# Seven products of quarters move from the second expert layer to the first, in a fixed order; V products and query pairs take turns

## The chip, the cores and the metric

The kernel runs on one core of one Trainium2 chip. A core has five engines that run side by side, each through its own list of instructions in order, and wait for each other by semaphores: TensorE (PE, the matmuls; PEld is its loading of the stationary operand), VectorE (DVE), ScalarE (ACT), GpSimd (POOL) and SyncE (SP, which here only starts transfers). The metric is the device time of one execution in microseconds (us), and a profiled execution gives a trace of every instruction.

## What is computed

Four sequences of 1024 tokens of width 256 (f32) go through a gated cross attention to 64 context tokens and a gated mixture of experts:

```python
x = x + tanh(g_xattn[0]) * xattn(layernorm(x), ctx, ctx, ...)
x = x + tanh(g_ffn[0]) * moe(layernorm(x), gate_w, w1, w2)

# xattn: 16 heads of 64
qh, kh, vh = (einsum('bld,hdk->hblk', t, w) for t, w in ((q, w_qs), (k, w_ks), (v, w_vs)))
attn = softmax(einsum('hblk,hbmk->hblm', qh, kh))
out = einsum('hblm,hbmk->hblk', attn, vh) * qh      # times the query once more
return concat_heads(out) @ w_proj.T + b_proj

# moe: 8 experts, F = 1024, the best two of each token
w_topk, sel = top_k(xt @ gate_w.T, 2); w_topk = softmax(w_topk)
h = silu(xt @ w1[e]); y = h @ w2[e]                 # for the chosen experts
out = sum over the two of w_topk * y
```

## The kernel before

**Attention.** The 4096 tokens are eight groups g of 512, each four tiles t of 128. The main loop goes over groups and tiles; at each tile it computes scores and softmax of the tile (`probabilities`), transposes the probabilities of the tile before, and does a share of the work of other groups: at t = 1 the V products of the group before (`attend`, matmuls L469 into PSUM tiles po, which VectorE multiplies by the query, L478) and then that tile's list of head pairs of the next group's queries (`queries`, matmuls L408 into pq, copied out by ScalarE, L416). `attend` works on two head pairs at a time, which take two PSUM banks. All these PSUM tiles come from one pool of four banks (`ps1`), used in turn; a pool of two tiles of two banks each (`ps2`) holds scores. In groups 2 to 6 two head pairs of queries stand at t = 1, in group 1 one, in 7 and 8 none.

**Experts.** Rows of tokens, sorted by expert, lie in a table in DRAM. They are worked off in slots; one slot has one expert's weights and so many rows. Slots 0 to 8 hold 256 tokens of the first half of the sequence and run partly beside attention. Slots 9 to 19 are wide: 9 to 14 ("sixes") hold 384 tokens, 15 to 19 ("fives") 320. Slots 20 to 28 hold 256 again. For each slot s, `run_slots` issues in this order: the first layer (`hidden`, L954 and L962: 8 blocks of F, two chunks of the contraction, Silu on ScalarE), the transpose of the tokens of slot s+1 (L928, VectorE), the second layer of slot s-1 (`combine`), the sums for slot s's own second layer (`quarter_sums`), and the loads of the weights of s+3 and the tokens of s+4 (SyncE's queue). An f32 matmul is two instructions in the trace. First-layer outputs use `ps2`, second-layer outputs `ps1`.

`combine` first makes the ids of the rows and their weights (L1040, L1043, VectorE, from small transfers that come with the tokens), multiplies, scales by the token's weight (L1088) and adds the rows to the output by a scatter of POOL (L1073). For the slots that `by_quarters` names (9 to 26) the product of two blocks of 128 tokens is done by seven products of quarters instead of eight (the Winograd form of Strassen's scheme): VectorE makes four sums of the hidden values (sh) and four of the weights (sw), each 128x512 (L987); `pair_of_blocks` does seven products of 128 columns (L1000), and the sums of products are made while leaving PSUM, on VectorE (L1010) and ScalarE (L1015, L1025). A third block of a wide slot is done plainly (L1109).

**What sets the order.** The program is written with a framework that inserts the semaphores and that may move instructions of an engine by priority and expected readiness. `pinned` (with a true second argument, or none) keeps an instruction in the order in which pinned instructions were written. Before, the expert layers aren't pinned. SBUF blocks come from three rings, "group" (8), "weight" (7) and "hidden" (2 buffers), and a new holder of a buffer waits for the last reader of the old. `kept` are eight long-lived tiles of input rows; slots put their token rows and their scaled results in them.

Of the kernel before, what the change touches and what calls it, by code (L numbers as in the profile page):

```python
# [8 lines left out]
F32 = mybir.dt.float32  # L9
# [6 lines left out]
P = 128  # L16
# [5 lines left out]
def kernel(  # L22
# [900 lines left out]
    def transposed(s, xin):  # L923
        blocks = xin.shape[1]
        n = S + HALF if is_half(s) else blocks * P
        pool, tag = (rows, "xT") if blocks == 2 else (npool, "nT")
        xT = pool.tile([P, NC, n], F32, tag=tag, name=f"xT_{s}")
        nc.vector.transpose(  # L928
            xT.rearrange("p c (i j) -> p i c j", j=Q),
            xin.rearrange("p t (i m c) -> p (t i) c m", c=NC, m=Q)[:, : n // Q],  # L930
        )
        return xT

    def hidden(s, a, xT):
# [27 lines left out]
            nc.scalar.activation(hT[f0 // per_tile][:, f1 : f1 + step, :], ph, AF.Silu)  # L962
            yield hT

    attention_ends = False

    def by_quarters(s):
        return NA <= s < NA + OFTEN - 2

    def quarter_sums(s, b, hT):  # L970

# [62 lines left out]
    def combine(s, ids, b, y, hT, sums):  # L1034

        blocks = ids.shape[1]
        n = tokens_of(s)
        of_rows = ids.bitcast(I32)
        with behind_sums():
            nc.vector.tensor_tensor(  # L1040
                of_rows[:, :, 0, 1:2], of_rows[:, :, 0, 1:2], of_rows[:, :, 1, 0:1], ALU.min
            )
            nc.vector.tensor_tensor(ids[:, :, 0, 0:1], ids[:, :, 0, 0:1], ids[:, :, 1, 1:2], ALU.add)  # L1043
            if is_half(s):
                half_row = of_rows[:, 2, 0, 1:2]
                nc.vector.tensor_tensor(half_row, half_row, half_row, ALU.add)
                nc.vector.tensor_tensor(half_row, half_row, second_half, ALU.add)
        behind = [f"slot{s - 1}"] if s else ["out0"]
        if s == NA:
            behind.append("out1")  # L1050
        gathered = None
        if s == NA + OFTEN - 1:
            gathered = flat[0]
            for t in range(blocks):
                gather = nc.gpsimd.indirect_dma_start(
                    out=gathered[:, t],
                    out_offset=None,
                    in_=outf[:n],
                    in_offset=bass.IndirectOffsetOnAxis(ap=of_rows[:, t, 0, 1:2], axis=0),
                    bounds_check=n - 1,  # L1060
                    oob_is_err=False,
                )
                apart("out", gather, behind=behind)

        def width(t):
            return D // 2 if t == 2 and is_half(s) else D

        def scatter(t):

            w = width(t)  # L1070
            rows_of = n * D // w
            with behind_softmax():
                rows_added = nc.gpsimd.indirect_dma_start(  # L1073
                    out=outf.rearrange("n (h d) -> (n h) d", d=w)[:rows_of],
                    out_offset=bass.IndirectOffsetOnAxis(ap=of_rows[:, t, 0, 1:2], axis=0),
                    in_=y[:, t, :w],
                    in_offset=None,
                    bounds_check=rows_of - 1,
                    oob_is_err=False,
                    compute_op=ALU.bypass if gathered is not None else ALU.add,  # L1080
                )
            apart("out", rows_added, f"slot{s}", behind=behind)

        def add(t):

            weight = ids[:, t, 0, 0:1]
            if gathered is None:
                nc.vector.tensor_scalar(y[:, t, : width(t)], py[t], weight, None, ALU.mult)  # L1088
            else:
                nc.vector.scalar_tensor_tensor(y[:, t], py[t], weight, gathered[:, t], ALU.mult, ALU.add)  # L1090
            scatter(t)

        each = attention_ends
        per_tile = NF // len(hT)
        alone = range(blocks)
        if sums:
            yield from pair_of_blocks(s, ids, y, sums, scatter)
            alone = range(2, blocks)
        if attention_ends:
            py = {t: bank(f"py_{s}_{t}")[:, : width(t)] for t in alone}  # L1100
        else:
            both = bank(f"py_{s}").rearrange("p (t d) -> p t d", d=D)
            py = [both[:, t, :] for t in range(blocks)]
        for t in alone:
            w = width(t)
            m = P * w // D
            for f in range(NF):
                for i in range(D // w):
                    nc.tensor.matmul(  # L1109
                        py[t][i * m : (i + 1) * m],  # L1110
                        hT[f // per_tile][:, f % per_tile, t * P : t * P + m],
                        b[:, f, i * w : (i + 1) * w],
                        start=(f == 0),
                        stop=(f == NF - 1),
                    )
            if each:
                add(t)
            yield
        if not each:
            for t in range(blocks):  # L1120
                add(t)
# [2 lines left out]

    def run_slots(slots):

        ahead = 3
        issued.clear()
        tokens, weights = {}, {}

        def load(s):
            if s in slots:
                weights[s] = load_weights(s)

        def load_next(s):
            if s in slots:
                tokens[s] = load_tokens(s)

        for s in slots[:ahead]:
            load(s)  # L1140
            load_next(s)
        load_next(slots[0] + ahead)
        yield
        yield
        xT = transposed(slots[0], tokens[slots[0]][1])
        yield
        pending = None
        for s in slots:
            a, b = weights.pop(s)
            ids, xin = tokens.pop(s)  # L1150
            if s == slots[-1] and pending:
                yield from combine(*pending)
                pending = None
            for hT in hidden(s, a, xT):
                yield
            if s + 1 in slots:
                xT = transposed(s + 1, tokens[s + 1][1])
                yield
            if pending:
                yield from combine(*pending)  # L1160
            pending = (s, ids, b, xin, hT, quarter_sums(s, b, hT) if by_quarters(s) else None)
            load(s + ahead)
            load_next(s + ahead + 1)
        yield from combine(*pending)


# [16 lines left out]
    def finish(g, step):  # L1183

        qT, aT = held[g]
        if step == 1:
            attend(g, range(NP // 2, NP), qT, aT)
        elif step >= 2:
            project(g, qT, (step - 2) * 2)

    def leave(g):
# [58 lines left out]
    for g in range(NG + 1):  # L1250
# [7 lines left out]
        for t in range(T):  # L1258
            if t == 0 and g >= 2:
                leave(g - 2)  # L1260
            if g < NG:
                pr = probabilities(g, t, qT)
            if last:
                transpose_probabilities(*last)

            b = (g - GB - 1) // GB
            ends, behind = b * GB + GB - 1, (g - GB - 1) % GB * T + t if b >= 0 else -1
            if behind == T:
                placing(ends)
            if g and t == 1:  # L1270
                attend(g - 1, range(NP // 2), *held[g - 1])
            for h, pairs in parts[g].items():
                queries(h, qTs[h], pairs[t])
            if 0 <= g - 1 < NG:
                finish(g - 1, t)
            last = (g, t, pr, aT) if g < NG else None
            if g == 0:
                for _ in range(value_parts[t]):
                    next(pending_values)
            if behind >= 0:  # L1280
                after(ends, behind)
            if g == 0 and t == 1:
                tc.keep_in_program_order(nc.scalar.activation(tg, tg, AF.Tanh))
                tc.keep_in_program_order(
                    nc.gpsimd.tensor_scalar(bias, bias, tg[:, 0:1], None, ALU.mult)
                )
                for h in range(2):
                    add_bias(h)
            if g + 2 < NG:
                if t == 0 and (g + 2) % GB == 0:  # L1290
                    stats = ln_stats(list(range(g + 2, g + 2 + GB)), f"a{g + 2}")
                elif t == 2:
                    ln_norm(g + 2, stats, "a")
                    add_bias(g + 2)
            if g < 2:
                clear(g * T + t, 2 * T)
            for _ in range(pieces[g][t] if g in pieces else 0):
                next(slots)
# [53 lines left out]
```

## Time and profile before

| | |
|---|---|
| median of 3 runs | 864.3 us (864.23 to 866.57) |
| profiled execution | 863.83 us, span 862.1 us |
| TensorE busy | 837.9 us (97%), 4684 instructions |
| VectorE / ScalarE / GpSimd busy | 462.6 / 237.7 / 269.2 us |
| first layer L954 | 928 instructions, 237.4 us |
| plain second layer L1109 | 608 instructions, 109.6 us |
| V products, multiply L478 | 64 of 128x512, 676 ns each |

Busy times of one engine's parts overlap with other engines', so only the engine that has no free time sets the end. A row of a group gives the number of its instructions, the summed busy time, the mean of one and the idle time of the engine just before them with what ended it; since matmuls are pipelined, the mean of one matmul is longer than the step to the next. The chain of waits lists, for an engine, which instruction of which other engine it waited for. The attention part ends about 450 us into the span; the wide slots fill TensorE from 521 to about 740 us.

### The profile page before, as it was taken

What the parts mean: (1) busy time and instruction counts of PE and PEld (TensorE: products, weight loads), DVE (VectorE), ACT (ScalarE), POOL (GpSimd) and SP (SyncE); (2) the same over time, 40 slices, a digit from 0 to 9 for tenths busy, and PEclk for the clock granted to TensorE, in tenths of its full rate; (3) what the DMA queues carried; (4) which work ended last, traced back from release to release, by engine and by line L of the source; (5) the groups of instructions that cost most, each with busy time, mean ns of one, the idle gap of its engine ahead of it and who ended that gap; (6) DMA issues with size and microseconds to landing.
All of it is one profiled execution on the core that took longest, in us unless ns stands there. A gap on an engine that the chain in (4) does not pass through costs nothing. (4 is left out here: it accounts for less than half of the span.)

```text
span 862.1 us, 13243 instructions
## 1 busy us (share of the span) xinstructions
PE 837.9 (97%) x4684; PEld 655.4 (76%) x4684; DVE 462.6 (54%) x1136; ACT 237.7 (28%) x380; POOL 269.2 (31%) x216
## 2 busy tenths in 40 slices
PE   8999999999999999899999999999999999999995
PEld 5556858576776758687888887777778888999995
DVE  4466384769647985864138611454344643645520
ACT  2673242333332231542113010212121211221210
POOL 3042212213731164215423722222222232223132
PEclk9999999999999999999999999999999999999999
DMA  9999999401200044336765888775555837856611
GB/s 197 334 341 340 340 345 340 132 2 43 74 32 1 25 159 115 115 79 210 207 192 138 219 207 195 209 175 133 136 129 136 234 91 177 232 130 183 172 23 38
DMA packets 165032, 141.79 MB, mean 164 GB/s; under 512 B 72685, under 2 KB 159076, under 8 KB 161248
## 3 DMA queue, kind: packets, MB, share of 16 engines
q1 hardware_dynamic: 145456, 118.79, 47.3%
q0 software_dynamic: 12912, 17.11, 10.2%
q10 hardware_dynamic: 6592, 4.98, 1.8%
q8 instruction: 39, 0.64, 0.3%
q14 instruction: 33, 0.27, 0.1%
HBM read 78.73 MB, written 62.46 MB: 164 GB/s over the span
## 5 line engine op out<-in xcount | busy, mean ns | idle before, releaser
L954 PE MATMUL ph<-xT,w 128*128 128x256 f32 (+2 forms) x928 | 237.4, 412 | 0.4 <-ACT hT L962 0.3
L954 PEld LDWEIGHTS ph<-xT,w 128*128 128x128 f32 x928 | 174.2, 190 | 51.9 <-issue 1.9
L1073 POOL DMA_INDIRECT out_dram<-x,ids x69 | 111.4, 1614 | 287.5 <-DVE x L1010 127.9
L962 ACT ACTIVATE hT<-ph 128x1024 f32<-128x1024 f32 (+3 forms) x84 | 70.1, 847 | 249.2 <-PE ph L954 211.9
L443 POOL TENSOR_TENSOR pr<-pr,sm 128x1024 f32<-128x1024 f32 x32 | 61.4, 1918 | 208.2 <-DVE sm L441 143.8
L408 PE MATMUL pq<-nT_a,wq 128*128 128x512 f32 x256 | 116.2, 597 | 5.7 <-DVE qT L478 5.4
L486 PE MATMUL pp<-wp,qT 128*128 128x256 f32 x512 | 113.1, 379 | 0.0
L486 PEld LDWEIGHTS pp<-wp,qT 128*128 128x128 f32 x512 | 97.1, 190 | 18.2 <-issue 5.7
L1109 PE MATMUL py<-w,hT 128*128 128x256 f32 (+1 forms) x608 | 109.6, 352 | 0.0
L1109 PEld LDWEIGHTS py<-w,hT 128*128 128x128 f32 (+1 forms) x608 | 93.1, 176 | 12.0
L408 PEld LDWEIGHTS pq<-nT_a,wq 128*128 128x128 f32 x256 | 46.2, 190 | 58.3 <-issue 43.8
L606 POOL DMA_INDIRECT table<-x,to_row x64 | 63.1, 985 | 42.7 <-DVE x L595 24.8
L424 PEld LDWEIGHTS sc<-keys,qT 128*128 128x128 f32 x512 | 62.6, 192 | 11.2 <-issue 10.8
L424 PE MATMUL sc<-keys,qT 128*128 128x128 f32 x512 | 67.1, 278 | 0.0
L455 ACT COPY aT<-pa 128x512 f32<-128x512 f32 x64 | 34.4, 591 | 82.1 <-PE pa L454 72.2
L433 DVE TENSOR_REDUCE mx<-sc 128x16 f32<-128x1024 f32 x32 | 39.0, 1217 | 28.0 <-PE sc L424 27.9
L440 DVE TENSOR_REDUCE sm<-pr 128x16 f32<-128x1024 f32 x32 | 39.0, 1218 | 23.9 <-ACT pr L438 23.8
L1000 PE MATMUL q<-sw,sh 128*128 128x128 f32 x432 | 51.7, 275 | 0.0
L1000 PEld LDWEIGHTS q<-sw,sh 128*128 128x128 f32 x432 | 50.2, 192 | 0.8
L1088 DVE TENSOR_SCALAR x<-py,ids 128x256 f32<-128x256 f32 (+1 forms) x31 | 14.2, 459 | 63.1 <-PE py L1109 63.1
L416 ACT COPY qT<-pq 128x512 f32<-128x512 f32 x64 | 36.4, 581 | 35.3 <-PE pq L408 35.1
L478 DVE TENSOR_TENSOR qT<-po,qT 128x512 f32<-128x512 f32 x64 | 40.6, 676 | 5.7 <-PE po L469 5.7
(261 smaller groups left out, 853.8 us busy)
## 6 DMA issues: line engine op xcount, KB each, us to landing
w<-in_L_ffn_w_dram SPq DMA_DIRECT2D x58, 1024.0 KB
table<-empty SPq DMA_DIRECT2D x8, 5016.0 KB
x<-table SPq DMA_DIRECT2D x116, 64.0 KB
out_dram<-x ACTq DMA_DIRECT2D x8, 512.0 KB
x<-in_x_dram SPq DMA_DIRECT2D x7, 512.0 KB
out_dram<-x,ids POOLq DMA_INDIRECT x69, 4.1
wq<-in_L_xattn_w_qs_dram SPq DMA_DIRECT2D x4, 256.0 KB
wv<-in_L_xattn_w_vs_dram SPq DMA_DIRECT2D x2, 512.0 KB
```

Of the source, the lines that this page charges most:

```text
L408: product = nc.tensor.matmul(pq, wq[:, c, p * P : (p + 1) * P], nT[g][:, c, :], start=(c == 0), stop=(c == NC - 1),)
L424: nc.tensor.matmul(sc[:, p // 2, :, p % 2, :], of_pair(qT, p)[:, t * P : (t + 1) * P], kT[g // GB][:, p, :], start=True, stop=True,)
L433: nc.vector.tensor_reduce(mx, scv, AX.X, ALU.max)
L443: nc.gpsimd.tensor_tensor(pr, pr, sm.unsqueeze(2).to_broadcast([P, H, M]), ALU.mult).ins,
L478: nc.vector.tensor_tensor(own, po[j], own, ALU.mult)
L486: nc.tensor.matmul(pp[:, i, :], of_pair(qT, p)[:, t * P : (t + 1) * P], wp[:, p, :], start=(p == 0), stop=(p == NP - 1),)
L606: nc.gpsimd.indirect_dma_start(out=table.rearrange("r (u w) -> (r u) w", w=2), out_offset=bass.IndirectOffsetOnAxis(ap=to_row[:, k, i : i ...
L954: nc.tensor.matmul(ph[:, i, :], a[:, c, f * P : (f + 1) * P], xT[:, c, :], start=(c == 0), stop=(c == NC - 1),)
L962: nc.scalar.activation(hT[f0 // per_tile][:, f1 : f1 + step, :], ph, AF.Silu)
L1000: nc.tensor.matmul(to, left[:, f, :], right[:, f, :], start=not onto and f == 0, stop=f == NF // 2 - 1, skip_group_check=onto,)
L1073: rows_added = nc.gpsimd.indirect_dma_start(out=outf.rearrange("n (h d) -> (n h) d", d=w)[:rows_of], out_offset=bass.IndirectOffsetOnAxis( ...
L1109: nc.tensor.matmul(py[t][i * m : (i + 1) * m], hT[f // per_tile][:, f % per_tile, t * P : t * P + m], b[:, f, i * w : (i + 1) * w], start= ...
```

## The change

1. The first layer of the wide slots (9 to 19) is done by seven products of quarters. `first_sums`, called right behind the transpose of the slot's tokens, makes four sums of weights (128x512, into a block of the "weight" ring) and four of tokens (128x192 or 128x160, into `kept[0]` or `kept[1]` in turn). `hidden_by_quarters` then works in two groups of four of the eight blocks of F; in each, seven products with half the tokens as columns go into four banks (two tiles of `ps2`), one copy on ScalarE and five additions on VectorE join them, and four Silu on ScalarE write the hidden values. The second group's first products reuse the first group's banks.
2. The second layer of the wide slots is plain; quarters remain there for slots 20 to 26.
3. In the wide slots the instructions of TensorE, the transposes, the additions and sums, the Silu and the scalings are pinned: their order on each engine is as written.
4. In attention, at t = 1, each two head pairs of V products are followed by one head pair of queries, so that po01, po23, pqA, pqB becomes po01, pqA, po23, pqB; po45 and po67 follow at t = 1 as well. Before, these were issued by `finish` behind the queries.

```diff
@@ transposed @@
-        nc.vector.transpose(
+        turn = nc.vector.transpose(
...
+        pinned(turn, in_order)
@@ new functions behind hidden @@
+    def first_sums(s, a, xT):
+        half = NF // 2 * P
+        sa = block([P, 4, half], f"sa_{s}", "weight")
+        w = [[a[:, c, f * half : (f + 1) * half] for c in range(NC)] for f in range(2)]
+        h = xT.shape[2] // 2
+        sx = kept[(s + 1) % 2][:, : 4 * h].rearrange("p (q n) -> p q n", n=h)
+        x = [[xT[:, c, t * h : (t + 1) * h] for t in range(2)] for c in range(NC)]
+        for out_, in0, in1, op in (
+            (sa[:, 0], w[1][0], w[1][1], ALU.add),
+            (sa[:, 1], sa[:, 0], w[0][0], ALU.subtract),
+            (sx[:, 0], x[0][1], x[0][0], ALU.subtract),
+            (sx[:, 1], x[1][1], sx[:, 0], ALU.subtract),
+            (sa[:, 2], w[0][0], w[1][0], ALU.subtract),
+            (sx[:, 2], x[1][1], x[0][1], ALU.subtract),
+            (sa[:, 3], w[0][1], sa[:, 1], ALU.subtract),
+            (sx[:, 3], x[1][0], sx[:, 1], ALU.subtract),
+        ):
+            pinned(nc.vector.tensor_tensor(out_, in0, in1, op), in_order)
+        return w, x, sa, sx
+
+    def hidden_by_quarters(s, n, sums):
+        w, x, sa, sx = sums
+        h = n // 2
+        share = "hidden" if s > NA and (s - NA) % 2 == 0 else "group"
+        hT = [block([P, NF // 2, n], f"hT_{s}_{i}", share) for i in range(2)]
+        per = 2
+        for f0 in range(0, NF // 2, per):
+            banks = [ps2.tile([P, 2, 512], F32, tag="ps2", name=f"ph_{s}_{f0}_{i}") for i in range(2)]
+            q = [banks[i // 2][:, i % 2, : per * h].rearrange("p (f n) -> p f n", n=h) for i in range(4)]
+            u = soft.tile([P, 2, per * h], F32, tag="pr", name=f"u_{s}_{f0}")
...
+            product(q[0], w[0][0], x[0][0])
+            pinned(nc.scalar.copy(u2, q[0]))
+            product(q[1], sa[:, 1], sx[:, 1])
+            plus(u2, q[1], u2)
+            product(q[2], sa[:, 2], sx[:, 2])
+            plus(u3, q[2], u2)
+            product(q[3], sa[:, 0], sx[:, 0])
+            plus(to[1][1], q[3], u3)
+            leave_hidden(1, 1)
+            product(q[0], w[0][1], x[1][0], True)
+            leave_hidden(0, 0, q[0])
+            product(q[2], w[1][1], sx[:, 3], True)
+            plus(to[1][0], q[2], u2)
+            leave_hidden(1, 0)
+            product(q[3], sa[:, 3], x[1][1], True)
+            plus(to[0][1], q[3], u2)
+            leave_hidden(0, 1)
+            yield hT
@@ by_quarters @@
-        return NA <= s < NA + OFTEN - 2
+        return NA + NW <= s < NA + OFTEN - 2
@@ combine: scalings and plain products @@
+                pinned(scaled, in_order)
...
+                    pinned(product, in_order)
@@ run_slots @@
+            in_order = is_wide(s)
-            for hT in hidden(s, a, xT):
+            for hT in hidden_by_quarters(s, xT.shape[2], first) if first else hidden(s, a, xT):
                 yield
+            first = None
             if s + 1 in slots:
                 xT = transposed(s + 1, tokens[s + 1][1])
+                if is_wide(s + 1):
+                    first = first_sums(s + 1, weights[s + 1][0], xT)
@@ finish and the main loop @@
-        if step == 1:
-            attend(g, range(NP // 2, NP), qT, aT)
-        elif step >= 2:
+        if step >= 2:
...
-            if g and t == 1:
-                attend(g - 1, range(NP // 2), *held[g - 1])
-            for h, pairs in parts[g].items():
-                queries(h, qTs[h], pairs[t])
+            asked = [(h, p) for h, pairs in parts[g].items() for p in pairs[t]]
+            for q in range(NP // 2):
+                if g and t == 1:
+                    attend(g - 1, range(2 * q, 2 * q + 2), *held[g - 1])
+                for h, p in asked[q : q + 1] if q + 1 < NP // 2 else asked[q:]:
+                    queries(h, qTs[h], [p])
```

More of the change, by code (lines that the diff above doesn't have):

```diff
@@ L963, in hidden @@
             yield hT
-    attention_ends = False
+    attention_ends = in_order = False
+    def first_sums(s, a, xT):
[17 more added lines that the diff above has]
+        return w, x, sa, sx
@@ new lines, in hidden_by_quarters, with product, plus, leave_hidden @@
+    def hidden_by_quarters(s, n, sums):
[8 more added lines that the diff above has]
+            u = soft.tile([P, 2, per * h], F32, tag="pr", name=f"u_{s}_{f0}")
+            u2, u3 = (u[:, i].rearrange("p (f n) -> p f n", n=h) for i in range(2))
+            to = [[hT[f][:, f0 : f0 + per, t * h : (t + 1) * h] for t in range(2)] for f in range(2)]
+            def product(to, left, right, onto=False):
+                for f in range(per):
+                    pinned(
+                        nc.tensor.matmul(
+                            to[:, f, :],
+                            left[:, (f0 + f) * P : (f0 + f + 1) * P],
+                            right,
+                            start=not onto and f == 0,
+                            stop=True,
+                            skip_group_check=onto or f > 0,
+                        )
+                    )
+            def plus(to, of, other):
+                pinned(nc.vector.tensor_tensor(to, of, other, ALU.add))
+            def leave_hidden(f, t, of=None):
+                pinned(nc.scalar.activation(to[f][t], to[f][t] if of is None else of, AF.Silu))
+            product(q[0], w[0][0], x[0][0])
[16 more added lines that the diff above has]
+            yield hT
@@ L1087, in add @@
             if gathered is None:
-                nc.vector.tensor_scalar(y[:, t, : width(t)], py[t], weight, None, ALU.mult)
+                scaled = nc.vector.tensor_scalar(y[:, t, : width(t)], py[t], weight, None, ALU.mult)
+                pinned(scaled, in_order)
             else:
@@ L1108, in combine @@
                 for i in range(D // w):
-                    nc.tensor.matmul(
+                    product = nc.tensor.matmul(
                         py[t][i * m : (i + 1) * m],
@@ L1125, in run_slots @@
     def run_slots(slots):
+        nonlocal in_order
         ahead = 3
@@ L1146, in run_slots @@
         yield
-        pending = None
+        pending = first = None
         for s in slots:
+            in_order = is_wide(s)
             a, b = weights.pop(s)
```

## The prediction

> **What bounds the kernel now.** I read the page's busy times first, then the chain of waits of TensorE, then its timeline, then the rows by shape.
>
> ```profile
> PE 837.9 (97%) x4684; PEld 655.4 (76%) x4684; DVE 462.6 (54%) x1136; ACT 237.7 (28%) x380; POOL 269.2 (31%) x216
> ```
>
> TensorE is busy for 97% of the span, so a change pays only by taking time or idle gaps from TensorE. Where the gaps are, the waits of TensorE say (total, times, longest):
>
> ```profile
> PE pq L408 <- DVE qT L478: 5.4, 6, 1.6
> PE pa L454 <- POOL pr L443: 2.1, 2, 1.3
> PE pt_b L317 <- DVE qT L478: 2.0, 4, 0.7
> PE po L469 <- DVE qT L478: 0.9, 1, 0.9
> PE ph L954 <- ACT hT L962: 0.3, 1, 0.3
> ```
>
> The 5.4 us in attention is what the reordering can reach. The expert layers have a single wait, of 0.3 us. TensorE's timeline in the wide slots (start, length, count) shows the pitch:
>
> ```profile
> 520.88 10.48 PE L954 MATMUL ph<-xT,w 128*128 128x384 f32 x32
> 531.20 7.07 PE L1109 MATMUL py<-w,hT 128*128 128x256 f32 x32
> ...
> 549.85 3.62 PE L1109 MATMUL py<-w,hT 128*128 128x256 f32 x16
> 553.30 15.64 PE L954 MATMUL ph<-xT,w 128*128 128x384 f32 x48
> 568.78 1.05 PE L1000 MATMUL q<-w,hT 128*128 128x128 f32 x8
> ...
> 638.65 8.78 PE L954 MATMUL ph<-xT,w 128*128 128x320 f32 x32
> 647.27 1.05 PE L1000 MATMUL q<-w,hT 128*128 128x128 f32 x8
> 648.16 2.84 PE L1000 MATMUL q<-sw,sh 128*128 128x128 f32 x24
> ```
>
> Start to next start, over the count: 384 columns 10.32/32 = 322.5 ns, 320 columns 8.62/32 = 269 ns, 256 columns 6.90/32 = 216 ns, 128 columns 0.89/8 = 111.5 ns. The price goes by columns. The mean in a row of groups (487 ns for 384 columns) holds the pipeline's depth and isn't used.
>
> **Part 1, first layer of the eleven wide slots.** 32 instructions (two for each f32 product) of 384 or 320 columns become 56 of 192 or 160. No row has these widths: the bounds are the 128-column row (111.5) and the 256-column row (216). The line through the wider rows gives 163 and 136 ns, the line between the bounds 164 and 138; I take 163.2 and 137. Six slots of 384 tokens: 56 x 0.1632 = 9.14 against 10.32, -1.18 each, -7.1. Five of 320: 56 x 0.137 = 7.67 against 8.62, -0.95 each, -4.7. Sum -11.8 us. One ns more per instruction is 616 ns over all. The outer bounds would give -36 us (56 x 0.1115 everywhere) and +28 us (56 x 0.216).
>
> The page "TensorE: Matmul & The Clock Gate" of the Trainium skill, section "Back-to-back issue gap", speaks against this part: in a stream of weight loads and matmuls the spacing comes from both, and falls slower than the columns (81 ns at 128, 131 at 512). Scaled by that line, 192 columns would cost 78% of 384, and 160 80% of 320: an estimate of 14.1 us for a six and 12.1 for a five, some +40 us instead of the gain. The trace has 111.5 against 322.5 for 128 against 384, which is near proportional, so the rows decide.
>
> **Part 2, second layer of the same slots.** For two token blocks, 56 instructions of 128 columns (6.25 us from 0.1115 each) become 32 of 256 columns (6.90): +0.65 x 11 = +7.2 us. The third block stays. TensorE's own work is so -11.8 + 7.2 = -4.6 us.
>
> **Part 3, what else moves.** On VectorE eight sums of 128x512 go (two rows carry their price):
>
> ```profile
> L987 DVE TENSOR_TENSOR sw<-w 128x512 f32<-128x512 f32 x36 | 24.5, 683 | 0.0
> L478 DVE TENSOR_TENSOR qT<-po,qT 128x512 f32<-128x512 f32 x64 | 40.6, 676 | 5.7 <-PE po L469 5.7
> L1010 DVE SCALAR_TENSOR_TENSOR x<-q,ids,q 128x128 f32<-128x128 f32 x54 | 18.7, 346 | 26.9 <-PE q L1000 26.9
> L1015 ACT ACTIVATE q<-q,ids 128x128 f32<-128x128 f32 x36 | 11.2, 366 | 52.7 <-PE q L1000 52.5
> ```
>
> In come four sums of weights, four narrow sums of tokens, and ten additions out of PSUM of 384 or 320 elements: between the rows of 676 and 346 ns, 566 and 511 ns. VectorE then has, by the steps between starts, 4 x 0.6 + 4 x 0.33 for sums, 10 x 0.55 for additions, 3 x 0.4 for scalings and 1.2 for transpose and ids: 11.6 us of work in a wide slot of 9.14 + 6.9 + 3.46 (third block) = 19.5 us. ScalarE does two copies and eight Silus of that size: between 366 and the 597 of its 128x512 Silu, 520 and 480 ns. None of this costs by itself; TensorE's matmuls cover it, unless it is late at a reuse.
>
> It is late at one place, the second group of a slot, whose first product rewrites the first group's first PSUM tile. For a six, with a product each 0.65 us and results seen 0.2 us behind (the 256-column block's next work starts at 553.30, its reader at 553.50): the fourth product ends at 2.61, is read at 2.81, its addition ends at 3.38, its Silu at 3.94, and the Silu of q0 behind it on ScalarE at 4.46. The seventh product ends at 4.57: just on time, and I charge 0.1 for the weight load that then isn't ahead. For a five (0.55 us a product): 2.19, 2.39, 2.90, 3.41, 3.89, against 3.84: 0.05 late, with hand-over and weight load 0.25. So 6 x 0.1 + 5 x 0.25 = +1.9 us. Ends: 0 (a gain is excluded, for there is no gap here now); above, 0.5 us at each of 22 groups, 11 us. Behind the waiting product stand all of TensorE's later work and so the end of the span.
>
> Slot 9 opens the new order. Its sums of tokens go into the buffer from which slot 6 scatters, and in VectorE's built order they stand around slot 6's second scaling. Before, the first of these scatters leaves POOL at 507.25 and lands 4.1 us later (the median of the scatters), at 511.4; then comes the first sum (0.3), the second scaling (0.4), and its scatter, which lands between 516.3, if it leaves at once, and 522, if POOL is held up as before its other scatters (1.9 to 7.7 us); three sums of 0.3 us follow. The second product is due at 522.3. So 0 to 0.7 us by this, at worst 3; I take +0.7.
>
> The ids (two operations of 0.16 us a slot) now stand between VectorE's pinned instructions and wait for tokens that SyncE's queue brings. The waits between 450 and 760 us say that they did wait before:
>
> ```profile
> DVE ids L1040 <- DMA x<-table: 9.8, 3, 3.8
> ```
>
> They are those of slots 9, 10 and 11, the last over at 523.84; from slot 12 on they found their tokens landed. In the built order they come earlier, within a slot's first layer; the tightest, of slot 13, would by my reading of the landings still find its tokens 1 us before its turn. Nothing, while that holds: if not, the additions stand behind them, and TensorE behind those, one for one. Weights are needed by VectorE some 10 us earlier than by TensorE; they land, by the loads' rows, about 20 us ahead. SyncE's weight loads wait less, as one block of sums per slot replaces two. The hidden tiles of slot 9 come from the ring of the weights of odd slots rather than from their own two; what held those buffers was read in attention, so this costs nothing. The fixed ScalarE and TensorE order moves no DMA; POOL's scatters follow the scalings, whose spare time is that of four PSUM banks.
>
> **Part 4, attention.** In groups 2 to 6 the order po01 po23 pqA pqB becomes po01 pqA po23 pqB. The gap sits where the first query product takes a PSUM bank that VectorE still reads:
>
> ```profile
> 308.38 1.95 PE L469 MATMUL po<-aT,vs 64*64 64x512 f32 x16
> 311.94 3.70 PE L408 MATMUL pq<-nT_a,wq 128*128 128x512 f32 x8 [1.62 <-DVE qT L478]
> 315.57 1.95 PE L469 MATMUL po<-aT,vs 64*64 64x512 f32 x16
> ```
>
> A query pair is 1.85 us of TensorE work that now comes while VectorE is still busy with row sums and multiplies its first two products. But the multiplications of po23 then start 1.85 us later behind VectorE's other work, and the wait returns at pqB or po45. Following the five regions: -0.5 (of 0.97), -0.5 (of 1.38), -0.95 (of 1.62), and +0.25 in the two regions with 0.49, where the normalization (L312) slips in ahead of po2. Sum -1.4 us; ends -6.3 (all waits of pq and po gone) and +1.
>
> **Sum.** -4.6 + 1.9 + 0.7 - 1.4 = -3.4 us against the profiled execution's 863.83 (span 862.1 and 1.7 around it): 860.4. That execution lies 0.5 below the median of 864.3, so 860.9 as a median.
>
> **Rivals.**
> *The waits don't come and attention gains more.* For it: VectorE has 8 us to spare in each slot, and a hand-over 0.1 us shorter than I took would clear the fives. Then -4.6 and -3 in attention: 856.7; with -6.3, 853.4. Against: the chain above leaves no slack.
> *Half-width matmuls are dearer than the line.* The widths aren't in the trace. At 4 to 8 ns over it (2.5 to 5 us) the gain is gone: 863.4 to 865.9. Against: four widths lie on one line within 2 ns.
> *Slower: the VectorE and ScalarE chain becomes the bound in each group.* Seven products now need five additions and a copy before their banks are free, with VectorE in a fixed order. It decides at 0.27 us more at each of the 22 groups (6 us, 866.9); 0.5 us at each, less the 1.9 counted, gives 870.0. For it: fives are already late by my working. Against: the additions' total, 2.8 us, is below a group's 4.6 or 3.8.
>
> **How the numbers follow.** A measurement of this kernel can tell about 0.3% (2.6 us) from no change: 861.7 and 866.9 are the bounds. My forecast, 858.5 to 863: 0.50, of which 0.38 lies below 861.7. More gain, 853.4 to 858.5: 0.19. Dearer columns, 863 to 866.9: 0.13. Slower by the chain: 0.18. Faster 0.57, same 0.25, slower 0.18. From 856.3 to 867.3 the range leaves out some 0.06 below and 0.14 above.
>
> **What would show it.** After, the first-layer products should start each 0.65 and 0.55 us; the second layer's blocks last 6.9 us without a wait; TensorE's waits should list products behind ScalarE's Silu, 0.1 to 0.3 us each, at every second group, one of at most 1 us at slot 9, and less than 4 us in all on the multiplications of attention. Waits of products behind VectorE's additions in most groups would prove the slower rival; one wait of several us behind ids would mean that I misread a landing; a pitch over 170 ns at 192 columns would prove the dearer columns.

## The result and the profile after

The changed kernel takes 928.3 us (median of 6 runs, 927.55 to 930.35) against 864.7 us for the kernel before (863.99 to 866.57). The ratio is 1.0737, with a 95% interval of 1.0725 to 1.0748. It is 63.6 us slower; the forecast was 860.9 us, with a range up to 867.3.

Its profiled execution has a span of 926.3 us. The busy times on the page of the changed kernel, and its chain of waits for TensorE (total, times, longest):

```profile
PE 861.9 (93%) x4684; PEld 678.7 (73%) x4684; DVE 496.8 (54%) x1202; ACT 243.7 (26%) x413; POOL 266.0 (29%) x216
```

```profile
PE ph L1006 <- DVE u L1017: 15.8, 22, 0.7
PE ph L1006 <- ACT u L1023: 15.8, 22, 0.9
PE ph L1006 <- DVE hT L1017: 13.6, 22, 0.7
```

The same number of TensorE instructions now takes 93% of a longer span. Three waits stand at the head, each 22 times, and there are 22 groups (two in each of the eleven wide slots). They sum to 45.2 us. None of them is the wait that the prediction counted (a Silu, L1020, at every second group).

TensorE's timeline in slot 10, the first of its two groups and the start of the second (start, length, count, and the idle time before it in brackets):

```profile
543.71 0.81 PE L1006 MATMUL ph<-xT,w 128*128 128x192 f32 x4
545.09 1.57 PE L1006 MATMUL ph<-x,sa 128*128 128x192 f32 x8 [0.57 <-ACT u L1023]
547.39 0.92 PE L1006 MATMUL ph<-x,sa 128*128 128x192 f32 x4 [0.73 <-DVE u L1017]
548.14 0.81 PE L1006 MATMUL ph<-xT,w 128*128 128x192 f32 x4
548.96 0.92 PE L1006 MATMUL ph<-x,w 128*128 128x192 f32 x4
550.53 0.92 PE L1006 MATMUL ph<-xT,sa 128*128 128x192 f32 x4 [0.65 <-DVE hT L1017]
551.28 0.81 PE L1006 MATMUL ph<-xT,w 128*128 128x192 f32 x4
```

A group takes 551.28 - 543.71 = 7.57 us where seven products of 0.65 us would take 4.55. A wait costs more than the idle time in brackets, since a matmul's modelled end lies some 0.16 us after the start of the next in a dense stream, and that overlap is lost too. Behind the first line the second product has to wait for the copy of the first one's result, although it writes another bank. The fourth waits for the addition that reads the third, the seventh for the addition that reads the sixth; the sixth starts at 548.96 rather than 548.79 for the same reason.

The whole slowdown lies there. A six's first layer takes 15.49 us (543.71 to the second layer at 559.20) against 10.32 before, a five's 13.78 (672.96 to 686.74) against 8.62. 6 x 5.17 + 5 x 5.16 + 11 x 0.65 for the plain second layer = 64.0 us, and the span grew by 64.2. At the first product of slot 9 the two traces stand 0.4 us apart.

### The profile page after: what moved, and what is told of

Same layout as the page of the kernel before. It is cut to its first block, busy times and chain, and to the rows that moved or that the text cites. A ratio compares the mean times of both kernels' runs of the same rounds, so it can differ in the third digit from the quotient of the medians.

```text
span 926.3 us, 13320 instructions
## 1 busy us (share of the span) xinstructions
PE 861.9 (93%) x4684; PEld 678.7 (73%) x4684; DVE 496.8 (54%) x1202; ACT 243.7 (26%) x413; POOL 266.0 (29%) x216
## 5 line engine op out<-in xcount | busy, mean ns | idle before, releaser
L1184 PE MATMUL py<-w,hT 128*128 128x256 f32 (+1 forms) x960 | 186.0, 362 | 0.0
L1184 PEld LDWEIGHTS py<-w,hT 128*128 128x128 f32 (+1 forms) x960 | 160.0, 181 | 21.7 <-issue 1.7
L955 PE MATMUL ph<-xT,w 128*128 128x256 f32 x576 | 129.5, 380 | 0.3 <-ACT hT L963 0.3
L955 PEld LDWEIGHTS ph<-xT,w 128*128 128x128 f32 x576 | 107.9, 190 | 15.9 <-issue 1.4
L963 ACT ACTIVATE hT<-ph 128x1024 f32<-128x1024 f32 (+1 forms) x40 | 37.2, 938 | 173.9 <-PE ph L955 141.2
L1006 PE MATMUL ph<-x,sa 128*128 128x192 f32 (+1 forms) x264 | 51.5, 331 | 31.7 <-DVE u L1017 15.8
L1006 PEld LDWEIGHTS ph<-x,sa 128*128 128x128 f32 x264 | 39.5, 189 | 43.6 <-DVE u L1017 21.8
L1017 DVE TENSOR_TENSOR hT<-ph,u 128x384 f32<-128x384 f32 (+1 forms) x66 | 34.8, 528 | 61.4 <-PE ph L1006 61.4
L1020 ACT ACTIVATE hT<-hT 128x384 f32<-128x384 f32 (+1 forms) x66 | 32.9, 499 | 117.4 <-DVE hT L1017 117.4
L1162 DVE TENSOR_SCALAR x<-py,ids 128x256 f32<-128x256 f32 (+1 forms) x53 | 24.7, 468 | 69.6 <-PE py L1184 69.6
```

Source lines behind the costliest of these rows:

```text
L955: nc.tensor.matmul(ph[:, i, :], a[:, c, f * P : (f + 1) * P], xT[:, c, :], start=(c == 0), stop=(c == NC - 1),)
L1006: nc.tensor.matmul(to[:, f, :], left[:, (f0 + f) * P : (f0 + f + 1) * P], right, start=not onto and f == 0, stop=True, skip_group_check=on ...
L1184: product = nc.tensor.matmul(py[t][i * m : (i + 1) * m], hT[f // per_tile][:, f % per_tile, t * P : t * P + m], b[:, f, i * w : (i + 1) * ...
```

## The experiments

They ran on two other chips, on which the kernel before takes 882.8 us (the first four runs) and 880.9 us (the others): TensorE's granted clock falls to 0.87 to 0.96 in stretches between 400 and 520 us there, with own tiles as with attention alone. So ratios are compared, each to the kernel before on the same chip. Where an expectation gives microseconds, multiply the ratio by 864.7.

One stretch can be compared in microseconds. From the first product of slot 9 to the first matmul of slot 20 the kernel before takes 203.83 us, and the run with attention alone, on another chip, takes 203.83 as well. The changed kernel takes 266.84 there, the other pairing 237.47, own tiles 200.69, and own tiles with the sums ahead 198.23.

**Each result in a tile of its own.** The first theory was that the built program makes a product wait for the readers of everything in its PSUM tile, and a tile here holds two banks with two products. The pools are exchanged, so that each product has a one-bank tile.

```diff
-            banks = [ps2.tile([P, 2, 512], F32, tag="ps2", name=f"ph_{s}_{f0}_{i}") for i in range(2)]
-            q = [banks[i // 2][:, i % 2, : per * h].rearrange(...) for i in range(4)]
+            banks = [bank(f"ph_{s}_{f0}_{i}") for i in range(4)]
+            q = [banks[i][:, : per * h].rearrange(...) for i in range(4)]
...
-            py = {t: bank(f"py_{s}_{t}")[:, : width(t)] for t in alone}
+            py = {t: bank(f"py_{s}_{t}", is_wide(s + 1))[:, : width(t)] for t in alone}
```

> The changed kernel, with each of the four PSUM results of a group in a tile of its own (one bank from the pool of four) instead of two to a tile; the second layer's results take the two-bank tiles meanwhile. Theory (the program makes a product wait for the readers of the other product of its tile): the three waits of each group go, a group of a six takes 4.6 to 4.8 us instead of 7.57, of a five 3.9 to 4.2, and the time is 858 to 868 us. Rival (the chain of copy, additions and Silu is too slow by itself, whatever the tiles): groups stay above 6.5 us and the time above 900 us.

Measured: 881.78 us against 882.76, ratio 0.9987 (0.9974 to 0.9999); times 864.7, 863.6 us. The timeline of TensorE in slot 11:

```profile
580.09 0.81 PE L1006 MATMUL ph<-xT,w 128*128 128x192 f32 x4
580.74 2.11 PE L1006 MATMUL ph<-x,sa 128*128 128x192 f32 x12
582.69 0.81 PE L1006 MATMUL ph<-xT,w 128*128 128x192 f32 x4
583.34 0.81 PE L1006 MATMUL ph<-x,w 128*128 128x192 f32 x4
583.99 0.81 PE L1006 MATMUL ph<-xT,sa 128*128 128x192 f32 x4
584.64 0.81 PE L1006 MATMUL ph<-xT,w 128*128 128x192 f32 x4
```

Not one wait is left in the group: 584.64 - 580.09 = 4.55 us, and 3.80 to 3.93 for the groups of a five. The additions, the copy and the Silu are the same instructions as in the changed kernel, so the rival (a chain too slow by itself) falls, and with it the slower rival of the prediction in the form it was put.

**Another pairing in the same tiles.**

```diff
-            q = [banks[i // 2][:, i % 2, : per * h].rearrange(...) for i in range(4)]
+            q = [banks[i % 2][:, i // 2, : per * h].rearrange(...) for i in range(4)]
```

> The changed kernel with one index changed: the products q0 and q2 share a tile, q1 and q3 the other, so that neighbours in the order never share. Theory (waits by tile): following the chain by tile, the third product waits for the copy, the fourth for the first addition, the fifth for the second, the sixth for the Silu of q0; a group of a six takes 6.0 us instead of 7.57, some 34 us less in 22 groups: 890 to 902 us. Rival (the chain is too slow by itself): the same additions in the same order, so no change, 926 to 930 us.

Measured, in one execution: 917.35 us, 1.0392 of 882.76, which is 898.6 us on the first chip's scale, within the theory's 890 to 902. The theory named four products that wait; in the timeline of one group only the last of them has idle time before it:

```profile
607.33 0.81 PE L1006 MATMUL ph<-xT,w 128*128 128x192 f32 x4
607.98 2.45 PE L1006 MATMUL ph<-x,sa 128*128 128x192 f32 x12
610.28 0.92 PE L1006 MATMUL ph<-xT,w 128*128 128x192 f32 x4
612.07 0.92 PE L1006 MATMUL ph<-x,w 128*128 128x192 f32 x4 [0.88 <-ACT hT L1020]
```

The sixth product (q2) waits for the Silu that reads q0, which now lies in its tile; the group takes 613.71 - 607.33 = 6.38 us, where the theory had 6.0. One index takes 29.4 us off the stretch from slot 9 to slot 20, where the chain by tile gave 34. The Trainium skill's page "PSUM — Partial Sum Buffer", section "PSUM bank collisions raise a hardware error", asks for a guard by bank and quadrant of partitions. q0 and q1 lie in two banks, so by that rule no wait was needed, and the run with own tiles has none; the program's wait was stricter than this rule.

**Without the fixed order.** The same two-bank tiles, nothing pinned in the wide slots (`in_order = False`, and `pinned` taken off the products, additions, copy and Silu of `hidden_by_quarters`).

> The changed kernel without the fixed order: the instructions of the wide slots are no longer pinned, the framework may put second-layer matmuls into the waits of the products. Rival (it is the fixed order that costs; the waits are harmless once they can be filled): 858 to 875 us. Theory (the tiles make the waits, and the order was settled before the waits are known): 885 to 928 us, with the same three waits in most groups.

Measured, in one execution: 901.74 us, 1.0215 of 882.76, 883.3 us on the first chip's scale. That lies between the two expectations. The timeline shows why:

```profile
561.88 0.81 PE L1006 MATMUL ph<-x,sa 128*128 128x192 f32 x4
562.53 0.59 PE L1184 MATMUL py<-w,hT 128*128 128x256 f32 x2
562.97 0.81 PE L1006 MATMUL ph<-x,sa 128*128 128x192 f32 x4
```

Second-layer matmuls (L1184) fill the waits. So most of the loss needs both: tiles that make the waits, and an order that lets nothing else run in them. Some 45 us (928.3 less 883.3) come back without the fixed order. Part of what stays is one place in slot 9: VectorE waits 3.3 and 7.2 us for scatters there, and TensorE stands idle for 6.7 us. The same place returns below, in own tiles without the fixed order.

**Attention alone.** The kernel before with the new order of V products and query pairs (the last two parts of the change's diff).

> The kernel before with the new order of V products and query pairs alone. The trace of the changed kernel, read at the same marks, gives -0.1 us over attention: 864.0 to 865.0 us, no difference. If the prediction's -1.4 us were right: 863.3 us.

Measured: 883.83 us, ratio 1.001 (0.9999 to 1.0021): no gain, at most 1.8 us lost.

**Two small losses taken out.** With own tiles a wait of 1.96 us was left in slot 10. VectorE's timeline there, in the run with own tiles:

```profile
554.91 0.48 DVE L1162 TENSOR_SCALAR x<-py,ids 128x256 f32<-128x256 f32 x1 [2.01 <-PE py L1184]
...
558.37 0.48 DVE L1162 TENSOR_SCALAR x<-py,ids 128x256 f32<-128x256 f32 x1 [2.83 <-PE py L1184]
558.77 0.68 DVE L986 TENSOR_TENSOR sa<-w 128x512 f32<-128x512 f32 x1
```

The sums of slot 10 stand behind slot 8's scalings, which wait for TensorE; TensorE's second product, due at 558.81, starts at 560.94. The source issues these sums ahead of those scalings, so at this place the order on the engine is not the written one; why is not shown. Issuing the scalings behind the sums (`summed` holds the last sum of the next slot), and attention as before, gives:

```diff
-                scaled = nc.vector.tensor_scalar(y[:, t, : width(t)], py[t], weight, None, ALU.mult)
+                with tc.issue_after(summed[-1]) if summed and in_order else nullcontext():
+                    scaled = nc.vector.tensor_scalar(y[:, t, : width(t)], py[t], weight, None, ALU.mult)
```

> The kernel with own tiles, and two of its small losses taken out: attention in the order of the kernel before, and the scalings of a slot issued behind the next slot's sums on VectorE, so that in slot 10 TensorE no longer waits 1.96 us for sums that stood behind a scaling. Theory (what is left of the change after the tiles is its own work on TensorE, -4.0 us, these two, and nothing else): 0.9945 to 0.9965 of the kernel before. Rival (something else in the changed order takes the gain): 0.998 to 1.001, as with own tiles alone.

Measured: 874.65 us against 880.94, ratio 0.9936 (0.9922 to 0.9949), 5.5 us on the first chip's scale: faster than both kernels, and slightly more than the theory, whose bound of 0.9945 lies within the interval. From the first product of slot 9 to the first matmul of slot 20 it takes 734.70 - 536.47 = 198.23 us, and the run with attention alone 744.68 - 540.85 = 203.83. These 5.6 us are TensorE's own work: the eleven first layers of the stretch take 93.6 us instead of 105.5 (11.9 less), its ten second layers 6.3 more. The theory's -4.0 us was too small because it set slot 15 before (8.62 us) against the later fives after (7.84), which took 8.72 before.

**Own tiles without the fixed order.**

> The run with the sums ahead, without the fixed order in the wide slots. Theory (the fixed order costs only because it can't fill waits, and with own tiles there are none): within 0.4% of the same kernel with the fixed order. Rival (the fixed order costs by itself): at least 1% faster than it.

Measured: 887.64 us, ratio 1.0082 (1.0065 to 1.0100), 1.5% slower than the run with the sums ahead. Both expectations fail. But this run lacks the sums ahead too, since the line above acts only where `in_order` is true. So its nearest partner with the fixed order is the run with own tiles (0.9987, with the new order in attention): about 1%, and 209.87 against 200.69 us from slot 9 to slot 20. Nearly all of that is the first layer of slot 9, which takes 18.08 us here (537.96 to 556.04) and 9.10 with the fixed order. VectorE's timeline in it, the two sums of tokens that wait:

```profile
542.61 0.36 DVE L988 TENSOR_TENSOR x<-xT 128x192 f32<-128x192 f32 x1 [3.54 <-DMA out_dram<-x,ids]
550.56 0.36 DVE L988 TENSOR_TENSOR x<-xT,x 128x192 f32<-128x192 f32 x1 [4.90 <-DMA out_dram<-x,ids]
```

These are sums of slot 10, which the framework put ahead of a scaling and of slot 9's additions. They wait for scatters. TensorE's fourth product then waits 3.3 us for a scaling that stands behind the first of them, and a later one 1.5 us for an addition behind the second. Between 540 and 550 us the granted clock is 0.66 besides, and products of 192 columns start each 1.28 us instead of 0.65. So the gain of the fixed order with own tiles is this one place; over the rest of the stretch the two runs differ by 0.2 us in sum (the run with own tiles has its wait at slot 10 there).

**Seven products in both layers.** `by_quarters` true for slots 9 to 26, the third block ahead of the seven products, the rest as in the run with the sums ahead.

> The run with the sums ahead, with seven products in the second layer of the wide slots as well, the third block ahead of them. TensorE's work falls by another 11 x 0.65 = 7.2 us, VectorE's rises to about 17 of 18.8 us in a wide slot, and its built order has four sums of second-layer weights (2.4 us) ahead of the next slot's additions. If VectorE can follow: 0.987. If these sums hold the additions up by 1 to 2 us in each slot: 0.998 to 1.01.

Measured: 883.49 us, ratio 1.0028 (1.0013 to 1.0042), the second of the two expectations. VectorE is busy 86% of the time between 600 and 700 us, and TensorE waits on its additions and on its sums of products (5.5 and 2.8 us in the list of waits). TensorE's work falls by 7.2 us by the expectation and the time rises by 0.9% over the run with the sums ahead; the list of waits explains part of that.

**The sums of weights on GpSimd.** The four sums of w1 and the four of w2 of a wide slot are issued to `nc.gpsimd`.

> The same with both layers, the eight sums of weights of a wide slot done by GpSimd instead of VectorE (4.8 us less on VectorE in each). If VectorE was the bound there: 0.986 to 0.990. If GpSimd's sums slow VectorE, or hold the scatters up so that the token loads come late: above 0.995.

Measured: 907.40 us, ratio 1.0306 (1.0289 to 1.0323), again the second expectation. Two of the rows by shape of GpSimd and VectorE in this run:

```profile
L1066 POOL TENSOR_TENSOR sw<-w,sw 128x512 f32<-128x512 f32 x22 | 39.3, 1785 | 0.2
...
L1066 DVE TENSOR_TENSOR sh<-sh,hT 128x512 f32<-128x512 f32 x18 | 31.6, 1757 | 0.0
```

A sum takes 1.5 to 1.8 us on GpSimd by its rows. On VectorE the four rows of sums of hidden values have means of 727, 757, 1335 and 1757 ns, where the run with both layers on VectorE has 682 to 685. The additions that read PSUM kept their 558 ns. That agrees with the Trainium skill's page "SBUF — State Buffer", section "SBUF: two separate sides", by which VectorE with two operands in SBUF and a GpSimd instruction that reads SBUF exclude each other for a whole instruction.

## Why the prediction was wrong

- **The step that failed** is in part 3: "It is late at one place, the second group of a slot, whose first product rewrites the first group's first PSUM tile." The working there let each product wait only for the readers of its own bank. As the runs show, it waits for the readers of its tile, and two products share one. The places are then three in each group: the copy before the second product, the second addition before the fourth, the fourth before the seventh. The eleven first layers take 162.2 us with these waits and 93.6 with own tiles: 3.1 us in each of 22 groups, 68.6 us in all, where +1.9 was charged. The prediction took the order of instructions from the built program and reasoned out the waits.
- **The slower rival** was put as the chain of VectorE and ScalarE becoming the bound in each group. Its price was to be 0.5 us a group and its chance 0.18. The place was right; the cause (work on these engines) and the size were not, as the own tiles show with the same work. Its sign, waits behind VectorE's additions in most groups, did come, and so that sign could not tell a slow chain from a shared tile.
- **Part 1 and part 2** were right. First-layer products start each 0.65 us in a six and 0.545 in a five; the first layer with own tiles takes 9.10 and 7.73 to 7.84 us (predicted 9.14 and 7.67). 105.5 - 93.6 = 11.9 us are gained, predicted 11.8, and the second layer costs the +0.65 per slot. TensorE's own saving is some -5.0, predicted -4.6. The prediction's estimate from the Trainium skill's page "TensorE: Matmul & The Clock Gate", section "Back-to-back issue gap", 14.1 us for a six, didn't come (9.10); the rows decided rightly.
- **The charged wait at the second group** (+1.9) is zero with own tiles. In a six the Silu of q0 ends 4.45 us after the group's start (584.54), as predicted (4.46), and the next group's first product starts at 584.64. In a five of the run with the sums ahead that Silu ends at 671.74 and the product starts at 671.67, so it does not wait for q0's reader; which bank it has the trace does not say.
- **Slot 9** (+0.7) and **the ids** (0): no wait of TensorE behind either in the changed kernel. What a moved VectorE instruction did cost was elsewhere, 1.96 us at slot 10 behind a scaling, and that only with own tiles.
- **Part 4** was wrong by its size. The waits of query products went from 5.4 us to nothing, as expected, and those of V products rose from 0.9 to 2.2. Between the same marks of the two traces groups 2 to 6 gained 0.61, lost 0.76, gained 0.27, lost 0.75 and gained 0.78: -0.15 us against -1.4 predicted. In groups 3 and 5 VectorE's order is now this (changed kernel):

```profile
167.19 0.25 DVE L441 RECIPROCAL sm<-sm 128x16 f32<-128x16 f32 x1
167.36 2.63 DVE L312 TENSOR_SCALAR x<-x,mv_b,rstd_b 128x256 f32<-128x256 f32 x3
169.91 1.27 DVE L478 TENSOR_TENSOR qT<-po,qT 128x512 f32<-128x512 f32 x2
```

Three normalizations of 2.6 us together slipped in ahead of the second pair of multiplications, as the prediction said, but it charged 0.25 us for that, and it was three times as much. The wait moved to the third V products (0.68 us each in groups 3 and 5).

With own tiles and the two small losses out the kernel gains 5.5 us: the waits are at zero, as in the prediction's first rival, but without its gain in attention. The step that turned -3.4 into +63.6 is the first one of this list: -5.0 of TensorE's own work and +68.6 of waits.

## What to carry to other kernels

Before pricing a stage that passes data between engines, find out for each instruction of one round which instruction releases it, from the built program or a first trace; here a tile that held two results made each wait for the other's reader. Give results that are consumed at different times tiles of their own before fixing an order by hand. A fixed order cost 5% here where products waited, because it let no other work run in the gap; with own tiles it was worth about 1%, because it kept the next slot's sums, which had to wait for a scatter, from standing ahead of this slot's scalings and additions.

## What the runs showed that was not expected

- The same fixed order has both signs: 1.0737 against 1.0215 with shared tiles (slower), 0.9987 against 1.0082 with own tiles (faster, by one place in slot 9).
- Reading the page alone hides part of a wait: the listed waits are 45.2 us, the groups lost 69. TensorE's busy time rose by 24 us (837.9 to 861.9) with the same count of instructions.
- A row of 128x512 sums on VectorE goes from 683 to as much as 1757 ns on the mean in the run where GpSimd does such sums.
